# Routed experts on tokens sorted by expert, through tables in HBM, in an adaLN transformer block

## The chip, the core and the metric

The kernel runs on one core of one Trainium2 chip. The metric is the device time of one execution in microseconds (us), as the median of several runs. A core has five engines with an instruction queue each: TensorE (matmuls, called PE in the profile, with the loads of stationary operands as PEld), VectorE (DVE), ScalarE (ACT), GpSimd (POOL) and SyncE (SP), and DMA engines that move data between HBM and on-chip memory (SBUF). Matmuls write to PSUM.

## The reference, cut to what matters

The input has B = 4 batches of T = 2048 tokens with C = 256 channels. Everything is fp32.

```
mod = silu(c) @ wmod                        # six vectors per batch: sa ca ga sb cb gb
h = layernorm(x) * (1 + ca) + sa
x = x + ga' * attention(h)                  # causal, 8 heads of 32, one extra rank-1 score term per head
h = layernorm(x) * (1 + cb) + sb
x = x + gb' * ffn(h)

ffn(xt):                                    # 8192 tokens
  shared = sum over 2 experts of  gelu(xt @ up_s) @ down_s
  probs  = softmax(xt @ router_w.T)         # 16 routed experts
  gate   = probs for the 4 largest, else 0
  routed = sum over 16 experts of  (gelu(xt @ up_r) * gate_r) @ down_r
  return shared + routed
```

Each expert maps 256 channels to 128 and back to 256. A token's gate is zero for 12 of the 16 routed experts.

## The kernel before

The tokens are cut into 16 blocks of 512 (`QB`), four for each batch. A block's 512 tokens are four subtiles of 128 (`TT` = 4). For each block i the program does, in this order:

- **Attention sums** (`sum_steps`, lines 340 to 414), for two groups of four heads. Step by step over the key blocks of 128 it computes scores (L358), subtracts the row maximum with one more small matmul (L368), masks the diagonal (L379), takes Exp (L382) and multiplies by V and by ones (L391). A block with index qb = i mod 4 in its batch has 4 (qb + 1) key blocks. At the end the sums are divided (reciprocal, L411).
- **The head**: `turned` (L237) transposes the normalized next block, `project` (L250 to L280) makes its q, k and v, `project_out` (L416 to L435) projects the attention result and adds it to x (the add runs on GpSimd, L435). `norm` (L214 to L229) is the layer norm: statistics on VectorE, a square root on ScalarE (L222), a reciprocal and the scaling on VectorE. The block is then turned, and `route` (L438 to L470) computes the router's logits (L442), softmax and the four largest.
- **The feed-forward (FFN) stage**: `expert_steps` (L473 to L536) runs all 18 experts (two shared, 16 routed) on all 512 tokens, two at a time: `ups` (L480, then Gelu, L488) and `downs` (L501), and VectorE adds each expert's result weighted by its gate (L513). All expert weights stay in SBUF (`upT`, `dnT`, L86 and L87).
- Into the FFN stage are merged the **maxima** of the next block (`max_steps`, L283 to L338): its scores (L298), the causal mask (L308) and the row maxima (L311) on VectorE. `merged` (L26) spreads two lists of steps evenly over one another. The first four steps of the maxima are emitted ahead of `turned` and `route`, to lie beside them (L572 and L573).

The order in which instructions are written is not quite the order in which they run: the framework's scheduler places an instruction ahead of earlier ones on its engine when it takes it to be ready sooner. It also places all waits, by the tiles that instructions read and write. On the chip each engine's queue is worked off in order.

A tile pool hands out a fixed number of buffers for each name, so a write waits until the buffer's last reader is done. PSUM has three double buffers `big` (scores, up results, turned blocks) and two buffers `acc` (attention sums, down results, project-out).

## Time and profile before

| what | value |
|---|---|
| median of 3 runs | 3286.05 us (3284.88 to 3286.93) |
| the profiled execution | 3284.37 us, span 3282.6 us from its first to its last instruction |
| mean granted TensorE clock in it | 0.907 of full speed |
| instructions | 38567 |
| moved by DMA | 26.60 MB |

The profile gives busy time and instructions of each engine, groups of instructions by source line with the idle time just before them and what released it, busy time by stretch, and a timeline. In a line such as `L311 DVE TENSOR_REDUCE parts<-ps ... x640 | 660.1, 1058 | 157.9 <-PE ps L298 151.4` the parts are: source line, engine, operation, the tile written and the tiles read, how often; busy us and mean ns of one; idle us of the engine before them, and which instruction ended most of that. Busy times of matmuls overlap, because they are pipelined; the pace of a stream is read from starts. DMA-issuing instructions aren't counted as busy. The granted clock falls to half for some microseconds when TensorE has been idle, as the profile's clock row shows (0.7 to 0.97 in the stages below).

One batch takes these stages in the profiled execution, in us, each cut at the first matmul of the next:

| block | attention sums | head | FFN with the maxima of the next block |
|---|---|---|---|
| 4 | 36.4 | 30.7 | 98.5 |
| 5 | 49.6 | 32.5 | 105.7 |
| 6 | 75.0 | 31.6 | 121.5 |
| 7 | 99.0 | 34.7 | 75.3 |

A gap of 1 to 10 us lies between an FFN stage and the next block's attention. Block 15 has no next block; from the end of its attention sums to the end of the program it takes 95.8 us.

### The profile page before, as it was taken

The page shows a single profiled execution, that of the slowest core. Times are in us where ns is not written, and L with a number is a line of the kernel's source. Part 1 is how long each engine was busy: PE and PEld are TensorE (multiplying, and loading weights), DVE is VectorE, ACT ScalarE, POOL GpSimd, SP SyncE. Part 2 cuts the span into 40 slices and gives each one's busy share as a digit, 9 for nine tenths or more (in the row PEclk, how much of TensorE's full clock was granted, in tenths as well). Part 3 has the DMA queues.
Part 4 walks back from the last instruction along what each step waited for, and adds up shares of the span by engine and source line. Part 5 has one row for each costly group of instructions (what it writes and reads, how often), then busy time and mean ns, then how long its engine had stood idle before and what let it go on. Part 6 is the DMA issues. An engine that isn't in the chain of part 4 may idle for free. (4 is left out here: it accounts for less than half of the span.)

```text
span 3282.6 us, 38567 instructions
## 1 busy us (share of the span) xinstructions
PE 2940.0 (90%) x16448; PEld 1374.1 (42%) x16448; DVE 1725.2 (53%) x3453; ACT 911.2 (28%) x1094; POOL 80.5 (2%) x60
## 2 busy tenths in 40 slices
PE   6889989989989989989998998988998998899888
PEld 3444424424444443432545343343254534334325
DVE  5564735823655582680456467276155646536524
ACT  1213142044222305106321321511622131241251
POOL 0000000000000000000000000000000000000000
PEclk8888988988989899899898989988988898899898
DMA  2000000000000000000000000000000000000000
GB/s 109 1 13 1 1 14 1 0 14 1 13 0 14 1 0 14 1 13 1 1 13 1 14 0 13 1 0 13 1 0 13 1 14 0 7 1 0 7 1 7
DMA packets 18603, 26.60 MB, mean 8 GB/s; under 512 B 1024, under 2 KB 17664, under 8 KB 18176
## 3 DMA queue, kind: packets, MB, share of 16 engines
q1 hardware_dynamic: 17456, 22.28, 2.0%
q8 instruction: 129, 2.11, 0.3%
q10 hardware_dynamic: 976, 1.86, 0.1%
q14 instruction: 42, 0.34, 0.0%
HBM read 15.75 MB, written 8.39 MB: 7 GB/s over the span
## 5 line engine op out<-in xcount | busy, mean ns | idle before, releaser
L311 DVE TENSOR_REDUCE parts<-ps 128x2 f32<-128x1024 f32 (+3 forms) x640 | 660.1, 1058 | 157.9 <-PE ps L298 151.4
L382 ACT ACTIVATE p<-st 128x1024 f32<-128x1024 f32 (+3 forms) x640 | 541.6, 893 | 716.2 <-PE st L368 514.7
L501 PE MATMUL pd<-dnT,act 128*128 128x256 f32 x2304 | 606.8, 401 | 81.4 <-DVE facc L513 81.3
L480 PE MATMUL pu<-hTb,upT 128*128 128x512 f32 x1152 | 581.2, 647 | 2.4 <-DVE parts L311 1.7
L513 DVE SCALAR_TENSOR_TENSOR facc<-pd,gate,facc 128x256 f32<-128x256 f32 x1024 | 474.1, 480 | 203.7 <-PE pd L501 189.4
L501 PEld LDWEIGHTS pd<-dnT,act 128*128 128x128 f32 x2304 | 420.2, 194 | 359.5 <-DVE facc L513 199.3
L298 PE MATMUL ps<-kT,qT 32*128 32x512 f32 (+3 forms) x2560 | 458.3, 616 | 78.6 <-DVE parts L311 65.9
L379 DVE TENSOR_TENSOR st<-st,kmask 128x256 f32<-128x256 f32 x256 | 98.6, 427 | 785.0 <-PE st L368 776.5
L488 ACT ACTIVATE act<-pu 128x1024 f32<-128x1024 f32 x144 | 147.5, 1024 | 1057.2 <-PE pu L480 1057.2
L358 PE MATMUL st<-qT,kT 32*128 32x512 f32 (+3 forms) x2560 | 399.4, 624 | 27.1 <-ACT p L382 27.1
L480 PEld LDWEIGHTS pu<-hTb,upT 128*128 128x128 f32 x1152 | 231.1, 207 | 250.0 <-issue 220.5
L391 PE MATMUL av<-p,vA 128*32 128x512 f32 (+3 forms) x2560 | 327.6, 569 | 0.1
L391 PE MATMUL dn<-p,ones 128*32 128x512 f32 (+3 forms) x2560 | 314.0, 553 | 0.0
L298 PEld LDWEIGHTS ps<-kT,qT 32*128 32x128 f32 x2560 | 153.9, 197 | 292.5 <-issue 153.6
L358 PEld LDWEIGHTS st<-qT,kT 32*128 32x128 f32 x2560 | 126.1, 199 | 294.0 <-issue 225.3
L391 PEld LDWEIGHTS dn<-p,ones 128*32 128x32 f32 x2560 | 88.7, 114 | 166.2 <-issue 157.1
L368 PE MATMUL st<-mT,unit 3*128 3x512 bf16 (+3 forms) x1280 | 140.0, 368 | 0.0
L308 DVE TENSOR_TENSOR ps<-ps,cmask 128x256 f32<-128x256 f32 x256 | 105.5, 424 | 61.7 <-PE ps L298 58.3
L391 PEld LDWEIGHTS av<-p,vA 128*32 128x32 f32 x2560 | 55.4, 110 | 186.0 <-issue 164.5
L327 PE MATMUL pr<-ident,pieces 128*128 128x128 f32 x128 | 24.8, 323 | 98.1 <-DVE pieces L322 98.1
L411 DVE RECIPROCAL rd<-rd 128x512 f32<-128x512 f32 x32 | 107.3, 3353 | 1.1
L525 POOL TENSOR_TENSOR facc<-facc,x 128x1024 f32<-128x1024 f32 x16 | 37.7, 2357 | 1873.0 <-issue 1635.2
(95 smaller groups left out, 1330.0 us busy)
## 6 DMA issues: line engine op xcount, KB each, us to landing
x<-in_x SPq DMA_DIRECT2D x16, 512.0 KB, 4.7
out<-facc SPq DMA_DIRECT2D x16, 512.0 KB, 3.2
upT<-in_up SPq DMA_DIRECT2D x1, 2304.0 KB, 17.8
dnT<-in_down SPq DMA_DIRECT2D x1, 2304.0 KB, 21.1
wm<-in_wmod ACTq DMA_DIRECT2D x1, 1536.0 KB, 11.3
wq<-in_w_qkv SPq DMA_DIRECT2D x1, 768.0 KB, 8.5
wo<-in_w_out ACTq DMA_DIRECT2D x1, 256.0 KB, 16.3
cT<-in_c ACTq DMA_DIRECT2D x1, 4.0 KB, 2.4
```

The lines of the kernel that those rows point to most:

```text
L298: nc.tensor.matmul(ps[:, u, :w], lhsT=qT[r : r + G, g, t * P : (t + 1) * P], rhs=kT[r : r + G, g, ch * QB : ch * QB + w], start=True, stop ...
L308: nc.vector.tensor_tensor(ps[:, :, w - P : w], ps[:, :, w - P : w], c_pair, ALU.add)
L311: nc.vector.tensor_reduce(parts[:, t, 2 * a : 2 * a + 2, ch], ps[:, :, :w], AX.X, ALU.max)
L358: nc.tensor.matmul(pair[h // 2][:, h % 2, lo:], lhsT=kT[r : r + G, g, kb * P : (kb + 1) * P], rhs=qT[r : r + G, g, lo:], start=True, stop= ...
L368: nc.tensor.matmul(pair[h // 2][:, h % 2, lo:], lhsT=unit3[r : r + 3, :], rhs=mT[r : r + 3, lo:], start=False, stop=True, tile_position=(r ...
L382: nc.scalar.activation(pt[:, 2 * a : 2 * a + 2, lo:], ps[:, :, lo:], AF.Exp)
L391: nc.tensor.matmul(dst[r : r + G, lo:], lhsT=vA[:, kb, c0 : c0 + G] if dst is acc else ones, rhs=pts[kb][:, h, lo:], start=(kb == 0), stop ...
L411: nc.vector.reciprocal(rd, rd)
L480: nc.tensor.matmul(pu[:, u, :], lhsT=upT[:, k, e + u, :], rhs=h2T[:, k, :], start=(k == 0), stop=(k == KC - 1),)
L488: nc.scalar.activation(act, pu, AF.Gelu)
L501: nc.tensor.matmul(pd[:, 0 if shared else u, :], lhsT=act[:, u, t * P : (t + 1) * P], rhs=dnT[:, e + u, :], start=not (shared and u), stop ...
L513: nc.vector.scalar_tensor_tensor(facc[:, t, :], pd[:, u, :], gate[:, t, r : r + 1], facc[:, t, :], ALU.mult, ALU.add,)
```

## The change

The routed experts no longer run on every token of a block. Blocks 0 to 14 form five groups of three (`GROUPS`); block 15 keeps all 16 routed experts on all its tokens (`dense_steps(last, True)`).

- **At the start** a table `experts` in HBM gets the routed weights, one row of 512 floats for each expert and partition; only the shared experts' weights stay in SBUF (`wsh`). Two buffers `xg` in HBM (64 x 128 rows each) are filled with zeros; `yg` (two), `h2d`, `gd` and `pre` are further tables in HBM.
- **`norm`** takes the inverse root with `pow` on GpSimd and no longer uses ScalarE. The norm of the next block is written behind both halves of the attention sums, no longer between them. `second_norm` is written at the end of a block's round; it applies scale and shift in two passes on GpSimd and writes the block to `h2d`.
- **`late_steps`** (merged into the next block's attention sums) turns the block, computes logits, softmax and the four largest, and counts: for each token and each of its four experts, the token's rank among the tokens of that expert, by matmuls with a triangle of ones (`earlier`) and with ones, and a running count `seen`.
- **`place_steps`**, once for each group: the counts, rounded up to tiles of 128 rows, give each expert's first row; `owner` says for each of 64 tiles which rows of `experts` it needs, `at` says for each token and choice its row. `scatter` then loads the three blocks from `h2d` and writes each token's row four times to `xg`, with 16 indirect transfers for each block.
- **`tile_steps`**, spread over the FFN stages of the next three rounds (a third each): for each pair of tiles it loads two tiles of `xg`, gathers the two experts' weights (one indirect transfer of 128 rows each), turns the tokens, runs up, Gelu and down and writes to `yg`.
- **`combine_steps`**, merged into the attention sums that follow: for each 128 tokens four indirect gathers from `yg`, a weighted sum, and the rest of the block's result from `pre`, which `dense_steps(i, False)` (the shared experts) has written.

The group of blocks 12 to 14 has no rounds after it: its tiles run after the loop, its combine beside block 15's experts. The core of the diff; places not shown follow from these (buffers are moved to pools with one buffer, `probs` has two buffers for three, `xs` is loaded one block ahead for two):

```
+    GROUPS = [list(range(n, n + 3)) for n in range(0, NBLK - 1, 3)]
+    MAXT = 3 * QB * TOPK // P + R
...
+    xg = [dram.tile([MAXT * P, C], F32, tag=f"xg{n}", name=f"xg{n}") for n in range(2)]
+    yg = [dram.tile([MAXT * P, C], F32, tag=f"yg{n}", name=f"yg{n}") for n in range(2)]
+    experts = dram.tile([R, P, 2 * C], F32, tag="experts", name="experts")
...
-        nc.scalar.activation(rs, rs, AF.Sqrt)
-        nc.vector.reciprocal(rs, rs)
+        nc.gpsimd.tensor_tensor(rs, rs, half_power, ALU.pow)
...
+        def scatter(j):
+            i = group.blocks[j]
+            rows = work.tile([P, TT, C], F32, tag="rows", name=f"rows{i}")
+            nc.sync.dma_start(
+                out=rows, in_=h2d[i * QB : (i + 1) * QB].rearrange("(t p) d -> p t d", p=P)
+            )
+            for t in range(TT):
+                for k in range(TOPK):
+                    nc.gpsimd.indirect_dma_start(
+                        out=xg[n % 2],
+                        out_offset=bass.IndirectOffsetOnAxis(
+                            ap=group.at[:, j * TT + t, k : k + 1], axis=0
+                        ),
+                        in_=rows[:, t, :],
+                        in_offset=None,
+                    )
...
+        def fetch(q):
+            xr = tiles.tile([P, 2, C], F32, tag="xr", name=f"xr{n}_{q}")
+            nc.sync.dma_start(
+                out=xr, in_=xg[n % 2][2 * q * P : (2 * q + 2) * P].rearrange("(u p) d -> p u d", p=P)
+            )
+            for u in range(2):
+                wt = tiles.tile([P, 2 * C], F32, tag=f"wt{u}", name=f"wt{n}_{q}_{u}")
+                j = 2 * q + u
+                nc.gpsimd.indirect_dma_start(
+                    out=wt,
+                    out_offset=None,
+                    in_=experts.rearrange("e p n -> (e p) n"),
+                    in_offset=bass.IndirectOffsetOnAxis(ap=group.owner[:, j : j + 1], axis=0),
+                )
...
+        def turn(q):
+            px = accp.tile([P, 2, KC, P], F32, tag="acc", name=f"px{n}_{q}")
+            for u in range(2):
+                for k in range(KC):
+                    nc.tensor.transpose(px[:, u, k, :], xts[q][:, u, k * P : (k + 1) * P], ident)
+            xt = tiles.tile([P, 2, KC, P], F32, tag="xt", name=f"xt{n}_{q}")
+            nc.scalar.copy(xt, px)
...
+        def step(q):
+            if q + 1 < pairs:
+                fetch(q + 1)
+            if q < pairs:
+                turn(q)
+            if 0 <= q - 2:
+                down(q - 2)
+            if 0 <= q - 1 < pairs:
+                up(q - 1)
...
     for i in range(NBLK):
-        load_x(i + 2)
+        load_x(i + 1)
+        if i % NB == 0:
+            gm[i // NB] = once.tile([P, 3, C], F32, tag="gm", name=f"gm{i}")
+            nc.sync.dma_start(out=gm[i // NB], in_=gd[i // NB])
         more = i + 1 < NBLK
...
+        steps_y = sum_steps(i, 0, qT, mTs[0], oT) + sum_steps(i, 1, qT, mTs[1], oT)
+        side = []
+        if i > 0:
+            if (i - 1) % 3 == 0:
+                groups.append(Group((i - 1) // 3, GROUPS[(i - 1) // 3]))
+            side += late_steps(i - 1, h2, groups[-1])
+        side = merged(side, ready)
+        ready = []
+        run(merged(steps_y, side))
         if more:
-            hT = turned(xn, (i + 1) // NB, 0, f"a{i + 1}")
+            xn = norm(xs[i + 1], f"a{i + 1}")
+            hT = turned(xn, (i + 1) // NB, f"a{i + 1}")
             qT = project(i + 1, hT)
         project_out(i, oT)
...
+        ffn = []
+        if i > 0:
+            ffn += dense_steps(i - 1, False)
+        if fill:
+            now, fill = fill[:share], fill[share:]
+            ffn += now
+            if not fill:
+                ready = combine_steps(filling)
+        if i > 0 and i % 3 == 0:
+            place = place_steps(groups[-1])
+            run(place[:3])
+            run(place[3:])
+            filling = groups[-1]
+            fill = tile_steps(filling)
+            share = -(-len(fill) // 3)
         if more:
             steps, mTs = maxima(i + 1, qT)
+            run(merged(steps, ffn))
+        else:
+            run(ffn)
+        h2 = second_norm(i)
+    last = NBLK - 1
+    tail = late_steps(last, h2, None)
+    run(merged(tail, ready))
+    run(fill)
+    run(merged(combine_steps(filling), dense_steps(last, True)))
```

## The prediction, made before the result was known

> **What bounds the kernel now.** I read the totals first, then the groups by line, then the busy time by stage, then short stretches of the timeline. The totals and the groups (busy us, mean ns of one, idle before it with its releaser):
>
> ```profile
> PE 2940.0 (90%) x16448; PEld 1374.1 (42%) x16448; DVE 1725.2 (53%) x3453; ACT 911.2 (28%) x1094; POOL 80.5 (2%) x60
> ...
> L311 DVE TENSOR_REDUCE parts<-ps 128x2 f32<-128x1024 f32 (+3 forms) x640 | 660.1, 1058 | 157.9 <-PE ps L298 151.4
> ...
> L501 PE MATMUL pd<-dnT,act 128*128 128x256 f32 x2304 | 606.8, 401 | 81.4 <-DVE facc L513 81.3
> L480 PE MATMUL pu<-hTb,upT 128*128 128x512 f32 x1152 | 581.2, 647 | 2.4 <-DVE parts L311 1.7
> L513 DVE SCALAR_TENSOR_TENSOR facc<-pd,gate,facc 128x256 f32<-128x256 f32 x1024 | 474.1, 480 | 203.7 <-PE pd L501 189.4
> ```
>
> TensorE bounds, and the expert matmuls (L480, L501) are its largest part. L501 has 2304 rows for 1152 matmul calls: each fp32 matmul runs as two instructions. GpSimd is nearly empty. One batch by stage, cut at the first matmul of each stage (stretch, its length, busy us of each engine, granted clock): attention of block 7, then the feed-forward (FFN) stages of blocks 4, 5, 6 and 7, then the tail behind the last attention sum.
>
> ```profile
> 1473.90:1572.90 99.00, 98.69 (x898) 28.84 (x897) 11.54 (x20) 57.86 (x66) 0.00 (x0) 0.96 0.03 8
> ...
> 937.20:1035.70 98.50, 91.68 (x331) 50.83 (x331) 62.73 (x138) 15.61 (x19) 0.00 (x0) 0.92 0.00 1
> ...
> 1120.90:1226.60 105.70, 97.50 (x395) 50.29 (x395) 76.35 (x143) 15.42 (x18) 0.00 (x0) 0.95 0.00 1
> ...
> 1342.70:1464.20 121.50, 112.56 (x459) 54.86 (x459) 94.85 (x163) 15.65 (x19) 0.00 (x0) 0.96 0.00 1
> ...
> 1607.60:1682.90 75.30, 74.70 (x267) 44.27 (x269) 45.22 (x125) 14.91 (x18) 0.00 (x0) 0.97 0.00 1
> ...
> 3186.80:3282.60 95.80, 77.21 (x257) 50.43 (x256) 42.76 (x102) 16.89 (x21) 4.86 (x3) 0.89 0.02 6
> ```
>
> Attention is pure TensorE (98.7 of 99.0). The FFN stages differ because each is merged with the maxima of the next block, whose VectorE load grows; VectorE is close behind TensorE in the longest (94.9 of 121.5). Between attention and FFN a head of 30.7 to 34.7 us turns, projects and routes. The pace of one instruction comes from starts in the timeline:
>
> ```profile
> 2923.57 0.66 PE L237 MATMUL pta<-ident,xna 128*128 128x128 f32 x4
> 2924.07 3.88 PE L254 MATMUL ppq<-hTa,wq 128*128 128x512 f32 x8
> ...
> 3217.17 3.62 PE L501 MATMUL pd<-dnT,act 128*128 128x256 f32 x16
> 3220.62 3.60 PE L480 MATMUL pu<-hTb,upT 128*128 128x512 f32 x8
> 3224.05 1.24 PE L501 MATMUL pd<-dnT,act 128*128 128x256 f32 x5
> ```
>
> Start to start: 0.125 us with 128 columns, 3.45/16 = 0.216 with 256, 3.43/8 = 0.429 with 512. All are with a weight load each.
>
> **The change, part by part.**
>
> *Experts leave the FFN stage.* For blocks 0 to 14 the routed experts issue no more 64 up instructions (27.5 us) and 128 down instructions (27.6): 55 us of TensorE per block. 64 L513 go too, 30 us of VectorE. *Tiles come instead.* Three blocks make 1536 x 4 rows = 48 full tiles of 128, plus one partial tile for each expert: 64 tiles, always computed, 320 in five groups. A pair of tiles costs 4 transposes and 8 up instructions at 0.125 and 4 down instructions at 0.216: 2.36 us. ScalarE has two copies of 128x512 (0.59 each by the num copy) and a half-size Gelu, under 1.8, beside it. A stage takes 12 pairs, 28 us.
>
> Now the stages of blocks 4, 5, 6, 7. TensorE work at full pace now: 62 of experts and 16/25/34/11 of maxima (score steps of 8 packed instructions in 1.14 us, 16 transposes, less the four steps in the head) = 78/87/96/73, so the stage is longer than its work by 20/19/25/2 (low clock, waits on PSUM). After: 55 less, 28 more, and the first four maxima steps, now in the head, join (4.6; little in the last): 55/64/73/46. VectorE: the busy column less 30, plus 10 for those steps, 2 for the shared experts' sums, 4 for the norm: 49/62/81/31. With the same slack on the larger: 75/83/106/48, a saving of 23/23/15/27. Blocks 4 to 14 have three of each of the first kinds and two of the last: 237 us. Blocks 0 to 3 have no tiles yet and fall to VectorE's figure: 69/81/106/33, saving 111. Together **-348**.
>
> *Attention takes over routing.* Transposes of h2 (8 x 0.125), 16 logits instructions and 14 for counting: 4.8 us on a full TensorE, 15 blocks: **+72**. The counting's VectorE work and, in one stage of three, the combine (per 128 tokens six passes of 0.4 to 0.5 us) lie beside it: VectorE has 11.5 of 99 us busy there. In the one-chunk block (36 us) that cover is thin.
>
> *The head shrinks.* Its work now at full pace is 23 us (project 11.1, project-out 3.5, both turns, logits, 4.6 maxima) in about 31. Without the last three it is 15.6, with the same 8 of gaps 23.6: -7.5, 15 times, **-112**. The norm of the next block no longer stands between the two halves of attention: if its chain (some 10 us: reciprocal 3.35, statistics, the pow on GpSimd, scaling) lies open, this is +45; if all gaps vanish, -170. I take the middle value because the program's scheduler moves ready work ahead: now the first norm runs at 4.5 us, ahead of the setup written before it, and project-out starts between two turns.
>
> *Start.* 16.8 MB of zeros and 4 MB of expert tables go into SyncE's queue before x of block 1. Packets of that queue took 2.0% of 16 engines' 3282.6 us for 22.28 MB, 340 GB/s: 62 us, so x1 lands at 70 to 95 us and is wanted near 86 to 100. **+15** (0 to 60).
>
> *GpSimd.* 800 indirect transfers: per group 48 scatters, 64 weight gathers, 48 row gathers. None is in the trace. From below: a plain transfer occupies SyncE's issue queue for 0.43 us. From above: each is paid until it lands, 2.4 us for the smallest (cT, 4 KB). I take 1.3 us, by the nearest row on GpSimd itself, one pass of 128x512 (1.26 us). At 1.3 a group costs 208 us of three blocks' 530, so it is hidden; at 2.4, 384, still hidden on average. But the norms' pow, project-out's add and the finish add queue behind transfers on GpSimd, VectorE waits for the pow, and TensorE for the norm. I take 2 us at each of 30 norms, **+60** (0 to 400). All 48 scatters write one table at places known only at run time; if the program orders them, each also waits for the landing before it, 1.3 + 2.0 = 3.3 us.
>
> A rule speaks against this part. The Trainium skill, "DMA: Bandwidth & Descriptors", section "Anatomy of one DMA — SWDGE (gpsimd) path", gives a transfer issued from GpSimd a fixed cost of about 2.0 us, most of it the wait for the write's receipt. If the queue paid that for each of the tail's 230 transfers, an estimate from that page is 160 us more than below and the change would lose; by the same page most of it is completion, not issue. No run here shows which yet.
>
> *SyncE* gets a load and a store for each pair; the store waits for ScalarE's copy and the next load stands behind it, but that load is a step ahead of its use: 0, at worst its landing (4.7 us for 512 KB of x) once a stage, inside the +60's bounds.
>
> *The tail.* Now 96 us. The last group has no attention to lie under. In GpSimd's queue, from 12 us before the attention sum's end: 48 scatters until 50, 22 weight gathers of the group before until 79, its 48 row gathers until 141, 64 weight gathers of the last group until 234 (10 more for first landings; TensorE needs 2.36 per pair, the gathers 2.6), 48 row gathers until 296, last sums and store 302. That is +206; with ordered scatters, whose waits hide other gathers, 334 or +238. I take **+225**. At 0.43 us it is bound by TensorE, +134; at 2.4 us the same chain ends at 556, +460. The last block's dense experts lie beside it; their weight loads, 256 KB each, are small.
>
> *Sum:* the profiled execution took 3284.4 us (span 3282.6). -348 + 72 - 112 + 15 + 60 + 225 = -88: 3196. The median of the runs is 1.7 above that execution: 3198, say **3200**. Sqrt and its 20 table loads leave ScalarE, which bounds nothing: 0 in the sum.
>
> **The rivals.**
>
> *A, GpSimd issues too slowly (slower).* The tail is a chain of 230 transfers; 85 us over the forecast is break-even, so it decides from 1.3 + 85/230 = 1.67 us each. At 2.4 us the tail gives +460: 3200 - 225 + 460 = 3435. For: each handles 128 separate rows, and no row of the trace shows one. Against: a whole GpSimd pass takes 1.26. Chance 0.24.
>
> *B, a new wait in the place of the old (slower).* Ordered scatters fill 48 x 3.3 = 158 us of GpSimd right at the norm and the last third of the tiles; the stage is only 48 to 106 us long, so some 75 us stay open at each of four groups: +300, 3500. It decides once a group's scatters take over about 100 us and are queued ahead of the pow. For: one table, four transfers for each 128 tokens. Against: the scheduler can queue ready work between. Chance 0.16.
>
> *C, more is gained.* Transfers near the lower bound, no norm waits, head without gaps: 134 in the tail, 0 for norms, -150 for the head: 3200 - 91 - 60 - 38 = 3011; with half of that, 3080. Chance 0.20.
>
> *D, nothing to measure:* gain and tail cancel, 3285. Chance 0.04. That the work is not removed can be ruled out: 320 + 64 tiles against 1024 are fixed in the program.
>
> **How the numbers follow.** Forecast 3200, chance 0.36, its own range 3120 to 3275. Faster by over 0.2% (about what a measurement of this kernel can tell from no change): 0.36 + 0.20 = 0.56; within 0.2%: 0.04; slower: 0.40. The range leaves out the lower end of C and the upper of A and B: 3040 to 3560.
>
> **What would show it.** Right: L513's successor only in the last block; FFN stages of 75 to 106 us; attention 5 us longer; indirect transfers near 1.3 us apart on GpSimd when nothing holds them; a tail near 320 us with GpSimd's queue unbroken in it. Wrong: gaps of TensorE before the turns with a GpSimd pow as releaser (B, and the +60); transfers over 1.67 us apart (A); tile instructions paced above 0.125 us; attention of block 0 waiting for x.

## The result, and the profile after

The changed kernel takes 3430.62 us (median of 4 runs, 3424.41 to 3438.04), the kernel before 3285.47 us on the same chip (4 runs). The ratio is 1.0443, with a 95% interval of 1.0416 to 1.047: slower by 4.4%, where faster was forecast. The profiled execution took 3438.04 us (span 3436.3).

The totals and the groups of the changed kernel's page that answer to those shown of before (busy us, mean ns of one, idle before it with its releaser):

```profile
PE 2668.0 (78%) x16359; PEld 1264.6 (37%) x16359; DVE 1531.3 (45%) x3141; ACT 952.2 (28%) x1310; POOL 965.7 (28%) x929
...
L380 DVE TENSOR_REDUCE parts<-ps 128x2 f32<-128x1024 f32 (+3 forms) x640 | 656.7, 1059 | 145.7 <-PE ps L367 133.6
...
L720 POOL DMA_INDIRECT wt<-experts,owner x320 | 306.9, 959 | 320.3 <-PE py L756 243.8
...
L692 POOL DMA_INDIRECT xg<-rows,at x240 | 236.3, 985 | 347.4 <-DMA xg<-rows,at 294.0
...
L742 PE MATMUL pu<-xt,wt 128*128 128x128 f32 x1280 | 211.4, 309 | 86.1 <-DMA wt<-experts,owner 70.4
...
L785 POOL DMA_INDIRECT got<-yg,at x240 | 232.9, 971 | 108.9 <-issue 70.4
```

The work did go: TensorE is busy 2668 us, 272 less than before, and L742 with its neighbours stands where L480, L501 and L513 stood. But TensorE's share fell from 90% to 78%: the time went into waits. An indirect transfer occupies GpSimd for 0.96 to 0.99 us, and nothing on the page says that this queue is full (28%). Only the scatters, L692, show a releaser that is a transfer of their own kind: each waits for the one before.

The same stages as before (stretch, its length, busy us of TensorE, its loads, VectorE, ScalarE and GpSimd, granted clock): attention of block 7, the FFN stages of blocks 4, 5, 6 and 7 behind their heads, and the tail behind the last attention sum.

```profile
1282.70:1452.80 170.10, 126.90 (x936) 36.24 (x936) 47.88 (x122) 59.17 (x68) 54.31 (x56) 0.77 0.24 72
768.00:872.70 104.70, 68.20 (x322) 39.21 (x320) 49.95 (x99) 17.39 (x31) 47.54 (x44) 0.71 0.45 145
936.00:1029.80 93.80, 78.33 (x419) 43.00 (x417) 68.27 (x114) 22.27 (x39) 34.51 (x31) 0.90 0.48 152
1122.00:1282.70 160.70, 112.25 (x453) 56.75 (x452) 93.20 (x146) 18.94 (x33) 72.91 (x70) 0.73 0.32 108
1467.70:1522.10 54.40, 44.45 (x262) 30.45 (x260) 32.69 (x83) 17.32 (x31) 28.81 (x25) 0.94 0.64 208
3007.20:3436.30 429.10, 212.07 (x953) 157.00 (x953) 106.87 (x264) 82.09 (x146) 229.65 (x231) 0.76 0.54 171
```

Two lines explain most of the loss. Attention of block 7 takes 170.1 us in place of 99.0: that is where the combine of the first group was put. Blocks 10 and 13 show the same, 157.3 for 74.8 and 142.1 for 49.5: together +246 (71, 82 and 93). The tail takes 429.1 in place of 95.8: +333. Summed over the blocks, head and FFN stages lose 454 us, attention gains 257 (the three stages above 246, all others together 11), the start 17, the tail 333: +153 us of span, which is the result.

Inside block 7's attention, in the timeline (start, duration, engine, idle before it):

```profile
1318.18 0.13 PEld L460 LDWEIGHTS av<-p,vA 128*32 128x32 f32 x1 [1.88 <-issue]
1318.24 0.95 POOL L785 DMA_INDIRECT got<-yg,at  x1 [0.30 <-issue]
1318.88 1.01 PE L460 MATMUL av<-p,vA 128*32 128x512 f32 x1 [0.41 <-issue]
1319.50 0.95 POOL L785 DMA_INDIRECT got<-yg,at  x1 [0.30 <-issue]
1319.60 0.13 PEld L460 LDWEIGHTS av<-p,vA 128*32 128x32 f32 x1 [1.30 <-issue]
...
1320.99 1.01 PE L460 MATMUL av<-p,vA 128*32 128x512 f32 x1 [1.10 <-issue]
...
1322.40 0.13 PEld L460 LDWEIGHTS av<-p,vA 128*32 128x32 f32 x1 [2.68 <-issue]
```

TensorE has work and waits for nothing that the profile names ("issue"), yet one instruction starts every 0.70, 0.72, 1.39 or 1.41 us: multiples of 0.70. At its normal pace it does 16 of L460's matmuls with their loads in 2 us; here they take 31. The granted clock is 0.50 from 1315 us on, but that is not the reason: at 0.50, at the start of this stage (1288.8 us), eight of them took 1.7 us. I call this the crawl. It falls into the time of the combine's gathers (GpSimd, 1302 to 1365 us, mostly 1.26 us apart). It is not TensorE's alone, as its end shows:

```profile
1357.42 1.01 PE L427 MATMUL st<-qT,kT 32*128 32x512 f32 x1 [1.80 <-issue]
1358.14 0.48 DVE L799 SCALAR_TENSOR_TENSOR sum<-got,weight,sum 128x256 f32<-128x256 f32 x1 [0.88 <-DVE sum L799]
1359.53 0.42 DVE L802 TENSOR_TENSOR sum<-sum,gbs 128x256 f32<-128x256 f32 x1 [0.91 <-issue]
...
1369.54 1.94 ACT L451 ACTIVATE p<-st 128x1024 f32<-128x1024 f32 x2 [53.93 <-remote]
```

From 1348 us on VectorE starts on the same step too. ScalarE's Exp (L451) waits 53.93 us, although TensorE started the last matmuls that it needs (L437) at 1315.5; "remote" says that no instruction in the profile was found to have ended the wait. So the first question was what the crawl hangs on.

### The profile page after: what moved, and what is told of

The parts are those of the page before. It is cut to its first block, busy times and chain, and to the rows that moved or that the text cites. A ratio compares the mean times of both kernels' runs of the same rounds, so it can differ in the third digit from the quotient of the medians.

```text
span 3436.3 us, 41465 instructions
## 1 busy us (share of the span) xinstructions
PE 2668.0 (78%) x16359; PEld 1264.6 (37%) x16359; DVE 1531.3 (45%) x3141; ACT 952.2 (28%) x1310; POOL 965.7 (28%) x929
## 4 chain that ended last, share of the span: by engine, by line
PE 24%; issue 10%; POOL 7%; DVE 6%; DMA 5%; another core or an unknown queue 1%; ACT 1%; POOLq 0%; SPq 0%; DVEq 0%; ACTq 0%
PE st L427 4%; PE av L460 4%; PE ps L367 4%; PE dn L460 3%; POOL got L785 3%; DVE parts L380 3%; DMA xg<-rows,at 2%; PE pu L742 2%; POOL wt L720 2%; PE py L756 2%; DMA wt<-experts,owner 1%; POOL xg L692 1%; PE px L733 1%; PE st L437 1%
## 5 line engine op out<-in xcount | busy, mean ns | idle before, releaser
L451 ACT ACTIVATE p<-st 128x1024 f32<-128x1024 f32 (+3 forms) x640 | 539.9, 894 | 690.9 <-PE st L437 297.3
L367 PE MATMUL ps<-kT,qT 32*128 32x512 f32 (+3 forms) x2560 | 594.4, 748 | 145.2 <-DVE parts L380 138.9
L720 POOL DMA_INDIRECT wt<-experts,owner x320 | 306.9, 959 | 320.3 <-PE py L756 243.8
L448 DVE TENSOR_TENSOR st<-st,kmask 128x256 f32<-128x256 f32 x256 | 98.6, 427 | 655.3 <-PE st L437 621.6
L460 PE MATMUL dn<-p,ones 128*32 128x512 f32 (+3 forms) x2560 | 337.4, 555 | 42.9 <-issue 42.6
L460 PE MATMUL av<-p,vA 128*32 128x512 f32 (+3 forms) x2560 | 341.2, 572 | 21.5 <-issue 15.2
L692 POOL DMA_INDIRECT xg<-rows,at x240 | 236.3, 985 | 347.4 <-DMA xg<-rows,at 294.0
L735 ACT COPY xt<-px 128x512 f32<-128x512 f32 x160 | 93.7, 586 | 738.3 <-PE px L733 709.2
L742 PE MATMUL pu<-xt,wt 128*128 128x128 f32 x1280 | 211.4, 309 | 86.1 <-DMA wt<-experts,owner 70.4
L785 POOL DMA_INDIRECT got<-yg,at x240 | 232.9, 971 | 108.9 <-issue 70.4
L733 PE MATMUL px<-ident,xr 128*128 128x128 f32 x640 | 115.8, 310 | 151.9 <-DMA xr<-xg 151.9
L742 PEld LDWEIGHTS pu<-xt,wt 128*128 128x128 f32 x1280 | 185.4, 214 | 129.2 <-issue 57.4
L756 PE MATMUL py<-wt,tact 128*128 128x256 f32 x640 | 190.0, 424 | 15.0 <-ACT tact L750 10.6
L460 PEld LDWEIGHTS dn<-p,ones 128*32 128x32 f32 x2560 | 91.6, 114 | 229.7 <-issue 221.0
L799 DVE SCALAR_TENSOR_TENSOR sum<-got,weight,sum 128x256 f32<-128x256 f32 x180 | 86.8, 483 | 163.5 <-DMA got<-yg,at 136.5
```

The costliest lines, as they stand in the source:

```text
L367: nc.tensor.matmul(ps[:, u, :w], lhsT=qT[r : r + G, g, t * P : (t + 1) * P], rhs=kT[r : r + G, g, ch * QB : ch * QB + w], start=True, stop ...
L451: nc.scalar.activation(pt[:, 2 * a : 2 * a + 2, lo:], ps[:, :, lo:], AF.Exp)
L460: nc.tensor.matmul(dst[r : r + G, lo:], lhsT=vA[:, kb, c0 : c0 + G] if dst is acc else ones, rhs=pts[kb][:, h, lo:], start=(kb == 0), stop ...
L692: nc.gpsimd.indirect_dma_start(out=xg[n % 2], out_offset=bass.IndirectOffsetOnAxis(ap=group.at[:, j * TT + t, k : k + 1], axis=0), in_=row ...
L720: nc.gpsimd.indirect_dma_start(out=wt, out_offset=None, in_=experts.rearrange("e p n -> (e p) n"), in_offset=bass.IndirectOffsetOnAxis(ap= ...
L733: nc.tensor.transpose(px[:, u, k, :], xts[q][:, u, k * P : (k + 1) * P], ident)
```

## The experiments

A number below is one run against a kernel before of 3281 to 3287 us on the same chip, unless an interval is given.

**Where the combine stands, and which part of it costs.** Four single edits of the changed kernel. `e1_combine_ffn` writes the combine into the next stage:

```diff
-        side = merged(side, ready)
-        ready = []
...
-        ffn = []
+        ffn = ready
+        ready = []
...
-            ffn += dense_steps(i - 1, False)
+            ffn = merged(dense_steps(i - 1, False), ffn)
```

> The twelve combine steps of a group are merged into the score and FFN stage of the same block instead of its attention sums; nothing else moves. Theory A (it is the neighbourhood of the attention sums that costs: VectorE's in-order queue and TensorE's crawl of 0.70 us steps belong to that stage): the sums of blocks 7, 10 and 13 fall back from 170, 157 and 142 us to about 100, 76 and 51, the stage after them grows by at most 60 us in all, time 3185 to 3250. Theory B (the gathers slow TensorE wherever they run): the sums fall back, but the score and FFN stages of the same blocks grow by about 70 us each, time 3390 to 3450.

Measured: 3432.8 us, nothing changed, but not for the reason of theory B. The sums of block 7 still took 167 us, and its gathers still ran inside them (1297 to 1359 us): the scheduler took them for ready and moved them, and the VectorE sums, back up. The edit did not move the work.

`e2_no_gather` reads zeros in place of the gathered rows:

```diff
-            got = work.tile([P, TOPK, C], F32, tag="got", name=f"got{i}_{t}")
-            for k in range(TOPK):
-                nc.gpsimd.indirect_dma_start(
...
+            got = zeros.unsqueeze(1).broadcast_to([P, TOPK, C])
```

> Leaves out the 240 gathers of the combine: its sums read a tile of zeros, so the routed share of the blocks 0 to 14 is missing from the output; the row loads, the VectorE sums and the stores stay where they are. Theory A1 (TensorE crawls because of the gathers): no crawl, the sums of blocks 7, 10, 13 at 100 to 105, 76 to 82, 51 to 57 us, the tail shorter by 60 to 100 us as well, time 3100 to 3180. Theory A2 (the loads of rows and the stores beside them, or VectorE's sums, make it crawl): the sums of these blocks stay above 130 us, time 3330 to 3390, most of the difference in the tail.

Measured: 3159.6 us; sums of blocks 7, 10 and 13 at 109, 81 and 54, no crawl, the tail 353. That is theory A1, but the edit took more away than the gathers: with nothing to wait for, the combine's VectorE sums were moved up by the scheduler as well, out of the attention sums into earlier FFN stages (those of the first group behind blocks 1 to 3). `e6` below tells the two apart.

`e3_no_row_out` takes the other transfers away:

```diff
-            row = tiles.tile([P, C], F32, tag="row", name=f"row{i}_{t}")
-            nc.sync.dma_start(out=row, in_=pre[at : at + P])
+            row = zeros
...
-            nc.sync.dma_start(out=of[at : at + P], in_=acc)
+            if n == len(GROUPS) - 1 or (j, t) == (len(group.blocks) - 1, TT - 1):
+                nc.sync.dma_start(out=of[at : at + P], in_=acc)
```

> Keeps the gathers and leaves out the combine's loads of rows (zeros are added in their place, so the attention and shared part is missing from blocks 0 to 14) and, but for the last group and one store per group, its stores (those rows of the output are not written). Theory A1 (gathers): the crawl stays, sums of 7, 10, 13 within 15 us of 170, 157 and 142, time 3400 to 3440. Theory A2 (the row loads and stores): no crawl, sums about 105, 80 and 55, time 3180 to 3240.

Measured: 3434.0 us, sums 169, 157 and 138, the crawl is there. It is not the row loads and stores; gathers and sums are left.

`e4_no_scatter` replaces the scatter call by `pass`.

> Leaves out the 240 scatters into the sorted tables, which then hold zeros: the routed tiles work on zeros, everything else stays. Theory S (the ordered scatters, 2.67 us apart alone, set the end of the stages they run in): blocks 6, 9 and 12 shorten by 25 to 50 us each and the tail by 90 to 140 us, time 3180 to 3280. Rival (in the blocks they are hidden, and in the tail the gathers of the fourth group would take 60 us of the same stretch anyway): only the tail gains, 60 to 80 us, time 3345 to 3375.

Measured: 3122.9 us, 308 less, more than the theory's bound. The tail lost 97, blocks 6, 9 and 12 lost 48, 40 and 30, but blocks 3, 4, 10 and 13 lost 12, 33, 26 and 31 as well: in the changed kernel the scatters run on into the stages behind, until 828 us in block 4's FFN stage, and until 1910 and 2564 us in the attention sums of blocks 10 and 13, among the gathers.

**What makes the gathers cost.** `e5_plain_loads` loads as many rows without indices:

```diff
-                nc.gpsimd.indirect_dma_start(
...
+                at0 = ((4 * j + t) * TOPK + k) * P
+                nc.sync.dma_start(out=got[:, k, :], in_=yg[n % 2][at0 : at0 + P])
```

> Replaces each gather of the combine by a plain load of 128 rows of the same table in their stored order, issued from SyncE: same bytes, same row size, same VectorE sums waiting for them, but the rows belong to other tokens, so the routed share of the output is wrong for the blocks 0 to 14. Theory G (indirect transfers issued by GpSimd beside the attention sums slow TensorE): no crawl, the sums of blocks 7, 10 and 13 at 105 to 110, 78 to 85 and 52 to 58 us, time 3160 to 3210. Theory T (the traffic itself, or VectorE standing in its queue on rows that are late): some crawl stays, as long as the rows take, 25 to 35 us for each group, sums at 130 to 145, 105 to 115, 80 to 90, time 3250 to 3330.

Measured: 3324.0 us. Sums 104, 77 and 54, no crawl, but this decides nothing between the theories: not one of these loads ran beside those sums. The rows that they read are fixed in the program, and the scheduler moved loads and VectorE sums up to where their tiles were written; of the first group's 48 loads, 18 start in the FFN stage of block 4, 24 in that of block 5 and 6 in that of block 6. Most stages behind attention grew by 14 to 28 us, those of blocks 4 and 5 among them, and so the time missed the forecast. What plain loads do beside the attention sums isn't shown.

`e6_gathers_alone` keeps the gathers and takes VectorE out:

```diff
-            nc.vector.tensor_scalar(acc, got[:, 0, :], weight[:, 0:1], None, ALU.mult)
...
-            nc.sync.dma_start(out=of[at : at + P], in_=acc)
+            for k in range(TOPK):
+                nc.sync.dma_start(out=of[at : at + P, k * 64 : (k + 1) * 64], in_=got[:, k, 0:64])
```

> Keeps the gathers and leaves out the combine's row loads and all its VectorE operations: a quarter of each gathered row is stored to the output as it is, so the blocks 0 to 14 of the output are not the sum. Theory V (TensorE is held because VectorE's in-order queue stands on the gathers, with work that TensorE needs behind it): no crawl and no stall, sums of 7, 10 and 13 at 105 to 112, 80 to 85, 52 to 58 us, time 3160 to 3220. Theory G or T (the transfers themselves slow TensorE): the crawl stays, sums above 145, 130 and 115 us, time 3370 to 3430.

Measured: 3422.8 us, sums 162, 149 and 134, with the crawl. VectorE's combine is not needed for the crawl, and the crawl alone is enough for most of the loss. With `e2`: without gathers no crawl, with gathers and without VectorE's sums there is one.

`e7_last_dense` leaves the fifth group out:

```diff
-    GROUPS = [list(range(n, n + 3)) for n in range(0, NBLK - 1, 3)]
+    GROUPS = [list(range(n, n + 3)) for n in range(0, NBLK - 4, 3)]
...
-            ffn += dense_steps(i - 1, False)
+            ffn += dense_steps(i - 1, i - 1 >= 3 * len(GROUPS))
```

> Only the blocks 0 to 11 are routed; 12, 13 and 14 run their experts dense, as 15 does, and the combine of the fourth group stands beside block 15's dense experts; the dense weights get tiles of their own, and five small tiles have two buffers in place of three. Theory (the tail is what the fifth group exposes: its scatters, its tiles and its combine): the tail falls from 429 us to 120 to 180, blocks 13 to 15 grow by 40 to 70 us each, the crawls of blocks 7 and 10 stay and that of 13 stays, time 3260 to 3340. Rival (the combine of the fourth group holds VectorE beside the dense experts, so the tail stays above 220 us): 3360 to 3420.

Measured: 3332.1 us, inside the theory's range (3260 to 3340); the tail fell to 222 (not to 180), blocks 13 and 14 grew by 54 each.

`e8_pinned_ffn` moves the combine for good. `keep_in_program_order` puts an instruction behind all that is already written on its engine:

```diff
+                tc.keep_in_program_order(
                     nc.gpsimd.indirect_dma_start(
...
+            tc.keep_in_program_order(
                 nc.vector.tensor_scalar(acc, got[:, 0, :], weight[:, 0:1], None, ALU.mult)
...
+        ffn = merged(ffn, mine)
```

> The combine is written into the score and FFN stage of the same block and its gathers and sums are pinned behind what is already written on their engines, so that the scheduler can't move them up into the attention sums; the gathers of a step stand one step ahead of its sums. Theory A (the loss belongs to the attention sums): the sums of 7, 10 and 13 fall to about 100, 76 and 51 us, the stages after them grow by at most 25 us each, time 3190 to 3260. Theory B (the gathers cost wherever they stand): those stages grow by 60 to 80 us each, time 3380 to 3440.

Measured: 3328.9 us, between the theories. Sums 106, 79 and 53, no crawl; the stages behind grew by 55, 25 and 43. There the gathers share GpSimd with the weight gathers and the norms' pow: one pow ran 35 us after its input was there. ScalarE's and VectorE's "remote" waits, none in the kernel before, come to 103 us in this run (198 in the changed kernel).

**Scatters, pace, and the parts together.** `e9_free_scatters` declares the scatters' targets disjoint:

```diff
+    xgv = [dram_disjoint_views(v, 3 * TT * TOPK) for v in xg]
...
-                        out=xg[n % 2],
+                        out=xgv[n % 2][(j * TT + t) * TOPK + k],
```

> The scatters of a group go through 48 views of the table that are declared disjoint, so that no scatter waits for the one before it; everything else stays. Theory S (the wait of a scatter for the landing of the one before it is what the scatters cost): they stand 1.25 to 1.35 us apart where nothing else is on GpSimd, the tail loses 50 to 75 us, the blocks 3, 6, 9 and 12 with their neighbours 80 to 170 us in all, time 3190 to 3300. Rival 1 (the rows themselves are slow to write): pitch above 2.2 us, time 3390 to 3430. Rival 2 (close together they slow TensorE as the gathers do): crawls or longer stages beside them take half of the gain back, time 3310 to 3380.

Measured: 3370.6 us. Two views, a scatter of the changed kernel in its tail and the waits of this kernel's scatters over the whole run (engine, tile, line, for whom, us, times, longest):

```profile
3155.06 0.97 POOL L692 DMA_INDIRECT xg<-rows,at  x1 [1.70 <-DMA xg<-rows,at]
```

```profile
POOL xg L694 <- issue: 69.1, 227, 0.3
```

Ordered, a scatter takes 0.97 us and waits 1.70 for the one before to land: 2.67 us apart. Free, it waits 0.3: 1.27 apart. That is the pitch of theory S, but the gain is 60 us, not 130 to 240: block 9 grew by 11 and block 12 by 22, and the tail fell only from 429 to 395 (blocks 10 and 13 lost 29 and 31). The time is that of rival 2 (3310 to 3380), and the trace speaks for it: in the FFN stages of blocks 9 and 12 VectorE waits 41 and 48 us for scores with "remote" as releaser. In the changed kernel, with the scatters 2.67 us apart or more, VectorE has no such wait in these stages.

`e10_paced_gathers` puts a pow on GpSimd behind each gather, so that in block 7 they stand 2.3 us apart; gathers and pow are both pinned to program order:

```diff
+                tc.keep_in_program_order(
+                    nc.gpsimd.tensor_tensor(pad2, pad, half_power, ALU.pow)
+                )
```

> Between two gathers of the combine GpSimd raises a constant of 128 by 4 elements to a power, about 1 us by its rows, so that the gathers stand about 2.6 us apart in place of 1.26; they stay beside the attention sums. Rate theory (TensorE is slowed when gathers follow one another faster than they can be worked off): no crawl, the sums of 7, 10 and 13 at 105 to 120, 80 to 95, 55 to 75 us, what is left of the gathers runs into the stage behind and costs 20 to 50 us there, time 3240 to 3340. Theory of a fixed price (each gather beside attention costs TensorE about 1.6 us): the sums of 7 at 155 or more, of 10 and 13 at 120 or more, and the rest behind them, time 3400 to 3480.

Measured: 3626.6 us, past both theories, and the most telling miss: no crawl at all, and yet sums of 197, 192 and 175. The waits of block 7's attention (engine, tile, line, for whom, us, times):

```profile
ACT rpr L574 <- DVE rpr L573: 89.1, 1, 89.1
...
PE st L431 <- DVE rpr L573: 84.3, 1, 84.3
```

L574 is the router's Exp. VectorE has all twelve combine steps in one run ahead of the router's maximum and L573; ScalarE has L574 ahead of the attention's next Exp; TensorE runs out of tiles. So a second cost lay under the crawl: the order of VectorE's queue.

`v1_pinned_dense` is e8 and e7 together, `v2_pinned_dense_free` adds e9.

> Two of the edits together: the combine pinned into the score and FFN stage, and the blocks 12 to 14 dense. If the two losses (the gathers beside the sums of blocks 7, 10 and 13, and the tail) are separate, the gains of 102 and 99 us add: 3220 to 3250. If the pinned combine of the fourth group and the dense experts of the last block hold one another up in the tail, the tail stays at 220 us or more with blocks 13 and 14 longer as well: 3270 to 3320.

Measured: 3208.4 us: both gains, and 22 more. It beats the kernel before by 2.4%.

> The two edits of the kernel before it, and scatters that don't wait for one another. If the wait among scatters sets the end of the stages of blocks 3, 6, 9 and 12, 80 to 130 us less than with the two edits alone: 3100 to 3160, faster than both kernels. If GpSimd's issue time (1.26 us for each transfer) takes its place as the limit of those stages: 3190 to 3230.

Measured: 3252.9 us, in neither range: the freed scatters make it slower by 44. Waits of block 12's FFN stage:

```profile
DVE ps L379 <- remote: 50.4, 2, 43.7
ACT xt L737 <- remote: 44.8, 2, 24.1
...
PE py L758 <- issue: 19.0, 1, 19.0
POOL xg L694 <- issue: 13.4, 44, 0.3
```

44 scatters stand back to back, 1.27 us apart, and the weight gathers of the last third of the tiles start only behind them; when each scatter waits, the gathers slip in between. But in that time TensorE's long waits are not for weights. They end with nothing named (7.9, 5.0 and 19.0 us, "issue"), and one of 19.2 us is for ScalarE's copy (L737), itself "remote"; VectorE's mask (L379) starts at 2387.8 us, 36 after the end of its scores (L369, 2351.9). `v1` has no "remote" wait in this stage. So close scatters bring stalls like those of the crawl, without its step of 0.70 us. How much of the 44 us is theirs and how much the place of the weight gathers isn't shown.

**Both costs at once.** `e11_pinned_attention` takes e8's pins and its gathers one step ahead, but leaves the combine in the attention stage, so its twelve steps are spread over the attention steps.

> The combine stays in the attention stage, but each step's first sum and its gathers are pinned behind what is written before them on their engines, and the gathers stand one step ahead of the sums, so that the twelve steps are spread over the attention sums instead of standing in one run ahead of the router's softmax on VectorE. Theory VQ (two costs that overlap: gathers back to back make TensorE crawl, and VectorE's run of twelve steps keeps the router's softmax, which ScalarE has in its queue ahead of the attention's Exp, waiting; spread out, neither remains): sums of 7, 10 and 13 at 105 to 120, 80 to 95 and 65 to 80 us, stages behind them as in the kernel after, time 3200 to 3260. Rival (any gather beside the attention sums costs TensorE its 1.6 us): sums above 150, 130 and 115 us, time 3390 to 3440.

Measured: 3248.9 us, sums 107, 100 and 117, no crawl. Block 7's attention in this kernel, to be set beside the first line of the stages above:

```profile
1276.80:1384.00 107.20, 104.29 (x939) 33.33 (x938) 44.89 (x118) 59.18 (x68) 53.83 (x56) 0.95 0.38 110
```

The same work on all engines, 63 us shorter, at a granted clock of 0.95 in place of 0.77: the cover that the prediction counted on exists. It also refutes the rate as the only condition: the gathers stand 1.3 us apart here too, in runs of 24 and 21.

`e12_pin_sums` pins only each step's first sum; `e14_ahead_unpinned` writes the gathers a step ahead and pins nothing.

> As the changed kernel, but the first sum of each combine step is pinned behind what is written before it on VectorE; the gathers stand in the same step and are left to the scheduler. If VectorE's order is what the stall hangs on (the run of twelve steps ahead of the router's softmax), the sums of 7, 10 and 13 fall as with both pinned, to 105 to 110, 95 to 105 and 110 to 120, without TensorE's steps of 0.70 us: 3240 to 3270. If the gathers' own place brings those steps, they stay with the gathers as dense as before: sums above 140, 125 and 125, time 3350 to 3430.

Measured: 3388.2 us, sums 161, 150 and 120, and the crawl is back.

> As the changed kernel, with the gathers (and the row load) of a combine step written one step ahead of its sums and nothing pinned: VectorE again has its twelve steps in one run. If writing the gathers ahead is what took TensorE's 0.70 us steps away, none are seen, TensorE goes on at full pace to the step behind the router's logits and waits there for VectorE until the run ends: sums of 7, 10 and 13 at 130 to 150, 110 to 140, 100 to 130, time 3340 to 3410. If the steps hang on something else, they are there again and the sums are as in the changed kernel, 3415 to 3440.

Measured: 3363.6 us, sums 147, 140 and 124, no crawl; block 7's attention holds the other cost alone, this time on the diagonal's mask (L448):

```profile
1369.51 0.42 DVE L811 TENSOR_TENSOR sum<-sum,row 128x256 f32<-128x256 f32 x1
1369.86 0.75 DVE L448 TENSOR_TENSOR st<-st,kmask 128x256 f32<-128x256 f32 x2
...
1370.32 1.94 ACT L451 ACTIVATE p<-st 128x1024 f32<-128x1024 f32 x2 [40.10 <-DVE st L448]
...
1371.39 1.01 PE L427 MATMUL st<-qT,kT 32*128 32x384 f32 x2 [37.36 <-ACT p L451]
```

Read backwards: TensorE waits 37 us for Exp, Exp 40 us for the mask, and the mask stands in VectorE's queue right behind the last add of the combine.

`v3_pinned_attn_dense` is e11 with e7; `v4_spread_two` also shares the steps of the later groups out over two attention stages:

```diff
-        side = merged(side, ready)
-        ready = []
+        now, ready = (ready, []) if i % NB == NB - 1 else (ready[:7], ready[7:])
+        side = merged(side, now)
```

> The spread combine in the attention stage, and the blocks 12 to 14 dense. Theory VQ: against the kernel with the combine pinned into the score stage (3208 us) the stages behind blocks 7, 10 and 13 lose about 55, 25 and 20 us and the sums gain 5 to 25 each: 3120 to 3180. Rival: 3300 to 3340, as with the blocks dense alone.

Measured: 3174.9 us (4 runs), ratio to the kernel before 0.9655 (0.9639 to 0.9671).

> As the kernel before it (combine pinned and spread in the attention stage, blocks 12 to 14 dense), but the twelve steps of the second and third group are shared out over the attention stages of two blocks, 10 and 11, 13 and 14. If what is left in the sums of blocks 10 and 13 (105 and 113 us for 75 and 50) is 48 transfers at 1.26 us that don't fit beside so short a stage, these fall to 75 to 85 and 55 to 75 us, the sums of 11 and 14 grow by at most 10 each, time 3105 to 3145. If the gathers cost what they cost wherever they stand beside attention, 11 and 14 grow by what 10 and 13 lose: 3165 to 3180.

Measured: 3154.6 us (4 runs, 3153.16 to 3155.92), ratio 0.9603 (0.9587 to 0.9619), the fastest kernel here. Sums of blocks 10 and 13 fell to 85 and 96, those of 11 and 14 did not grow: a lack of room, not a price per gather. The time is 10 us above its range: the stages behind blocks 10 and 13 grew by 7 and 10. Block 13 missed its 55 to 75 because the next group's scatters run on into it (to 2402 us, the stage is 2325 to 2421) and the pinned gathers queue with them. Its totals:

```profile
PE 2650.2 (84%) x16380; PEld 1261.9 (40%) x16380; DVE 1574.0 (50%) x3207; ACT 931.4 (30%) x1250; POOL 813.7 (26%) x769
```

TensorE is busy about as long as in the changed kernel (2668 us); what was recovered is waiting.

## Why the prediction was wrong, step by step

| Step | predicted | measured |
|---|---|---|
| head and FFN stages of blocks 0 to 14 (-348 - 112 + 60) | -400 | -454 |
| attention takes over routing and combine | +72 | +257 |
| start | +15 | +17 |
| tail | +225 | +333 |
| sum | -88 | +153 |

*What held.* The experts' work left as worked out. From the end of attention to the next block, blocks 0 to 3 took 361 us in all, where the times of before (545) less the forecast savings of stages and head leave 405; blocks 4, 5, 8, 10, 13 and 14 took 677, where they leave 721, and blocks 7 and 11 took 145, where they leave 136. That the row comes out at -454 for -400 is partly luck: these stages beat the savings by 79 us, and those of blocks 6, 9 and 12 (rival B, below) fell behind them by 85, with +60 set down for all of GpSimd's waits. The head shrank more than I took: 14.9 us from the sums' end to the end of project-out, not 23.6. Routing beside attention cost less than 4.8 us a block: the thirteen stages without a combine grew by 11 us together (those of blocks 4, 8 and 12 shrank by 1 to 6 each, for a reason not looked into). Indirect transfers issue 1.26 us apart; I had said 1.3. Rival A, which gave 3435, is refuted although its number is near the result: it needs over 1.67 us each.

*The step that failed first* is this one of the prediction: "the combine ... lie beside it: VectorE has 11.5 of 99 us busy there." I looked at busy time, and it was free. The combine was put at nothing in these stages, and they grew by 246. What the cover lacked was order. The combine's sums wait for transfers, and an instruction that waits held all behind it in VectorE's queue: the router's maximum and the attention's mask (e10: 89 us, e14: 40 us of ScalarE's wait). On top came the crawl, which nothing in the trace of before could show. The two overlap, so each alone costs most of block 7's 63 us over e11 (e6: crawl alone, sums 162; e14: order alone, 147; both, 170; neither, e11, 107), and removing one shows little. In the changed kernel itself the crawl hides the other cost: ScalarE's longest wait for VectorE in block 7's attention is 4.3 us. The prediction asked of GpSimd's queue what stands behind a transfer there, and did not ask it of VectorE's.

*The second is the size of the tail,* +333 for +225, inside its bounds. The scatters were ordered, the case I had priced at +238. Their waits did hide other transfers, but these ran out: from 3020 us to 3152, 13 us behind the sums' end, GpSimd issues 22 scatters with 22 weight gathers and the 48 gathers of the fourth group between them, some 1.3 us apart, up to four gathers to a scatter. Then 26 scatters stand alone, 2.67 us each, until 3222. The last group's first tile starts 218 us after the sums' end. That is not the whole miss: against the +238 the scatters end 42 us late, 25 of them because the first one stood 13 us behind the sums' end and not 12 ahead of it; the last tiles took 20 us more (113 for 93) and the last combine with the end 33 more (101 for 68). The tail by stretch (scatters with gathers, scatters alone, tiles, last combine):

```profile
3020.00:3152.00 132.00, 40.19 (x197) 32.10 (x196) 36.92 (x104) 20.43 (x35) 97.73 (x96) 0.66 0.58 179
3152.00:3222.00 70.00, 0.00 (x0) 0.00 (x0) 1.91 (x5) 0.00 (x0) 25.07 (x27) 0.50 0.16 57
3222.00:3335.00 113.00, 92.19 (x513) 75.12 (x514) 0.00 (x0) 48.78 (x95) 54.93 (x58) 0.91 0.89 291
3335.00:3436.30 101.30, 69.39 (x209) 43.33 (x207) 55.43 (x137) 10.17 (x13) 49.24 (x49) 0.85 0.42 129
```

For 70 us TensorE and ScalarE do nothing, and VectorE 1.9 us of work, behind one queue of waits.

*Rival B* was half right. The ordered scatters take the whole gain of the stages they run in: from attention's end to the next block, blocks 6, 9 and 12 take 175, 148 and 122 us, 445 together, for 443 before and 360 by the forecast savings. But the norm was not the path: VectorE waited for pow 71 us in 27 waits in the whole run, while TensorE in these three stages waited 17, 15 and 21 us for weight gathers (L742), which stand among the scatters in GpSimd's queue. Leaving the scatters out gives 308 us. How much of that is the wait between them isn't shown: taking it away gave 60 us (e9) or cost 44 (v2), but brought stalls of its own.

The Trainium skill, "DMA: Bandwidth & Descriptors", section "Anatomy of one DMA — SWDGE (gpsimd) path", gives a fixed 2.0 us and 436 GB/s; for 128 KB an estimate from that page is 2.3 us. The run shows 2.67 us between scatters that wait for one another and 1.26 us between gathers that don't: the fixed cost is near what a dependent transfer pays, and the queue does not pay it.

## What to carry to other kernels

Idle time of an engine is cover only for instructions that don't wait: before work with transfers in it is put beside something else, list what stands behind it on each in-order queue it uses, and spread it with its loads a step ahead. When two costs overlap, undoing one proves little; look for the run in which both are gone. And a scheduler that moves ready work up can undo an edit of the source, so read from the trace where the work really ran before a theory is judged by it.

## What the runs showed of the hardware that was not expected

The crawl: beside the gathers, TensorE's attention instructions start on a step of 0.70 us, one to three steps apart, in the changed kernel for 17 to 43 us at a time, while GpSimd goes on at its own pace. VectorE joins it late (in block 7 from 1348 to 1369 us). In e6, where VectorE has no combine, SyncE shares it: stores that occupy its queue for 0.34 us take 0.70. It is there in every kernel in which the gathers run beside the attention sums 1.26 us apart and are written in the same step as their sums (the changed kernel, e1, e3, e4, e6, e7, e9, e12). The step is not there with gathers written a step ahead (e8, v1 and v2 in another stage, and e11, e14, v3 and v4 beside attention in runs at the same 1.3 us), with the gathers pinned and a pow between (e10), or in the changed kernel's tail beside dense experts.

Its wider sign, "remote" waits of ScalarE and VectorE, goes further: they come to 198 us in the changed kernel, 479 in e9, 346 in v2, 103 in e8 and 79 in v1, and to none in the kernel before, e11, e14, v3 and v4. So indirect transfers 1.26 us apart can hold other engines up in the FFN stages too, and need not do it beside attention. Neither the rate nor the bytes explain that alone (e11 and e14 have both), nor do VectorE's sums (e6) or SyncE's row loads (e3). What it is in the chip stays open; so does whether the recording has a part in it, since every run here was recorded.
